# A reordered opening for a dequantizing feed-forward kernel: first-tile copies, rescales and statistics

## The chip, the cores and the metric

The kernel runs on one core of one Trainium2 chip. The metric is the device time of one execution in microseconds. A core has TensorE (PE, with its weight loads PEld), VectorE (DVE), ScalarE (ACT), GpSimd (POOL) and SyncE (SP). SP, ACT and GpSimd can each issue DMA transfers from a queue of their own; within a queue instructions are issued in order.

## The reference, cut to what matters

The input is 2 x 1024 rows of 1024 numbers, so 2048 rows. Three residual steps follow each other:

```python
x = x + 0.5 * ffn(layernorm(x))
x = x + s4(layernorm(x))
x = x + 0.5 * ffn(layernorm(x))
# ffn: h = silu(xf @ Wg) * (xf @ Wu); out = h @ Wd
# weights: W[k,n] = scales[g[k],n] * (w4[k,n] - (z4[g[k],n] + 1))
```

Wg and Wu are 1024 x 2752, Wd is 2752 x 1024. They come packed, eight 4-bit numbers in one 32-bit word, with a scale and a 4-bit zero point for each group of 128 rows of k and each column. The step in the middle, s4, convolves each row of 1024 with a response that is computed from a few small tables.

## The kernel before, in words

**Tiling.** The rows are worked through in four blocks of 512. A job is one block with one feed-forward step, and there are eight jobs, (0,1), (1,1), (0,3), (1,3), (2,1), (3,1), (2,3), (3,3): block, and 1 or 3 for the first or second feed-forward step. Each job has an **up stage** (`gate_up`, the products with Wg and Wu) and a **down stage** (`down`, the products with Wd). The s4 step of a block is laid into a later up stage.

**The weights are unpacked once.** During the first job the packed words are fetched, split into bytes (`split`, L381 and L382: the low and the high halves of every byte), and `dequantize` (L396) subtracts the zero point and writes a tile q of integers as floats. q goes to HBM (L400, tensors `wq`), and the products read it back from there as tiles w (L461). All later jobs only read. The same is done for Wd (`dequantize_down` L428, stores L430, loads L469). The scales are not multiplied in; instead a sum in PSUM is multiplied between two groups g and g+1 by the ratio of their scales (`scaled`: on ACT L477, on DVE L479), and by the last scale at the end (L523, L526).

**Waves and steps.** The up stage has eight waves of three or two column tiles of 128, and each wave eight steps g, 64 steps in all. A step has six pairs of products, one for each unit (a column tile of Wg or of Wu): with the low part (xTl) and with the high part (xTh) of the rows, both 512 wide (L501). The six sums of a wave lie in six PSUM banks. After each step but the last each unit is rescaled: units with an even number on ACT, the others on DVE, except that in job 0 the unit at position 1 is also ACT's when `g % 4 < 3`. The down stage has 44 steps of four units (L562), with the same kind of rescale.

**The buffers.** One pool of six tiles (`wpool`) holds both the q on their way to HBM and the w that were read back, and the first tile. A load of w is issued `AHEAD = 3` steps before its products.

**The first tile.** The first step's weights don't take the way through HBM: while q of wave 0 is written, the 16 partitions of q that belong to group 0 are copied from one buffer to the other, eight times 48 KB, with DMAs from ACT's queue (L399, `first_tile`).

**The opening.** In the order of the program: the zero points of all three matrices are fetched, unpacked (L220, L229), stored in HBM as a table and read back spread over the rows (L376); four tiles x of rows come in (L1163); `moments` (L137, L138) takes mean and variance of each tile and ACT subtracts the mean (L1173); `deviations` (L156 to L159) works out the reciprocal deviation r with three Newton steps on tiles of four columns; eight times `dequantize`; the first scale table (`scales`); ACT multiplies by r (L1185); TensorE transposes (L173), ACT rounds the result to the high part (L187) and DVE takes the rest as the low part (L188).

**What sets the order.** The program attaches pieces of work to steps (`at(up, s, f)`, `at(dn, s, f)`), but a planner then orders the instructions of each engine by when it thinks their operands are ready and their result is due. Work written for a later step can so come to stand earlier: the statistics of job 1's rows are written for step 0 of the first down stage, and ran from 194.9 us on, within the first up stage; the small operations on `s_vc`, which begin the tables of s4 and are written for job 1, ran from 314.8 us on in the first down stage.

Of the kernel before, what the change touches and what calls it, by code (L numbers as in the profile page):

```python
# [15 lines left out]
ALU = mybir.AluOpType  # L16
AX = mybir.AxisListType
PSUM = bass.MemoryType.PSUM
DRAM = bass.MemoryType.DRAM
# [30 lines left out]
def macaron_s4_kernel(  # L50
# [63 lines left out]
    shift_t = const.tile([P, 1], I32, tag="shift", name="shift_t")  # L114


    x = {}
# [50 lines left out]

    def turned(n, half, name, bank=bank):

        ps = bank(name)
        for k in range(4):
            nc.tensor.transpose(ps[:, bass.ts(k, P)], n[:, bass.ts(4 * half + k, P)], ident)  # L173
        return ps.rearrange("p (c t) -> p c t", c=4)
# [4 lines left out]
    def turn(b, t, n, half, bank=bank):  # L179
        k = ln[b, t][2]  # L180
        if b not in pieces:
            pieces[b] = [
                xtpool.tile([P, NC, TB], F32R, tag="xT", name=f"xT{w}_{b}_{k}") for w in ("h", "l")
            ]
        hi, lo = (a[:, 4 * half : 4 * half + 4, bass.ts(t, P)] for a in pieces[b])
        ps = turned(n, half, f"pt_{b}_{k}_{t}_{half}", bank)
        nc.scalar.copy(hi, ps)  # L187
        nc.vector.tensor_tensor(lo, ps, hi.bitcast(F32), ALU.subtract)  # L188
# [19 lines left out]

    def zero_points():

        n, nd = INTER // 8 // SEG, HID // 8 // SEGD
        z = t2("zq").bitcast(I32)[:, : n + nd]
        nc.gpsimd.memset(z, 0)
        for i, src in enumerate((gate_qz, up_qz)):
            own = slice(GK * SEG * i, GK * SEG * (i + 1))
            nc.scalar.dma_start(z[own, :n], src.rearrange("g (s n) -> (g s) n", s=SEG))
        nc.scalar.dma_start(z[: GD * SEGD, n:], down_qz.rearrange("g (s n) -> (g s) n", s=SEGD))
        zi = t4("zi").bitcast(I32)[:, : 8 * (n + nd)]
        for k in range(8):
            nc.vector.tensor_scalar(  # L220
                zi.rearrange("p (a k) -> p k a", k=8)[:, k, :],
                z,
                4 * k,
                15,
                ALU.logical_shift_right,
                ALU.bitwise_and,
            )
        tab = t2("ztab").bitcast(BF16)[:, : 8 * (n + nd)]
        nc.vector.tensor_scalar(tab, zi, 1.0, None, ALU.add)  # L229
        nc.scalar.dma_start(z_dram.rearrange("g (s n) -> (g s) n", s=SEG), tab[:, : 8 * n])  # L230
        nc.scalar.dma_start(
            zd_dram.rearrange("g (s n) -> (g s) n", s=SEGD), tab[: GD * SEGD, 8 * n :]
        )

# [156 lines left out]
    def dequantize(w, j):  # L391

        parts, z = packed[w]
        q = wpool.tile([P, width_of(w)], F32R, tag="w", name=f"q_{w}_{j}")
        src = parts[j % 2][:, j // 2, :]
        nc.vector.tensor_tensor(q, src, z, ALU.subtract)  # L396
        dst = w_q[w].rearrange("(r j) n -> j r n", j=8)[j]
        if w == 0:
            nc.scalar.dma_start(first_tile[j:P:8].bitcast(F32), q[: P // 8].bitcast(F32))  # L399
        nc.sync.dma_start(dst, q.bitcast(F32))  # L400
        if j == 7:
            packed.pop(w)
# [31 lines left out]
    def first_weights(up, dn, at):  # L434


        for w in range(1, len(WAVES)):
            s0 = 8 * w - 12
            at(up, max(0, s0 - 3), lambda w=w: (fetch(w), fetch_zeros(w)))
            at(up, max(0, s0 - 1), lambda w=w: split(w))  # L440
            for j in range(8):
                s = s0 + j if w > 1 else (1, 2, 2, 3, 3, 3, 4, 4)[j]
                at(up, s, lambda w=w, j=j: dequantize(w, j))
# [9 lines left out]

    AHEAD = 3

    def load_w(j, s):
# [24 lines left out]
    def gate_up(j, b, hooks):  # L481
        hi, lo = pieces[b]
        ps = {}
        ready = {s: load_w(j, s) for s in range(AHEAD)}
        for s, (wi, g) in enumerate(STEPS):
            if s + AHEAD < len(STEPS):
                ready[s + AHEAD] = load_w(j, s + AHEAD)
            for hook in hooks.get(s, ()):
# [7 lines left out]
            for pos, (unit, col) in enumerate(order):  # L496
# [12 lines left out]
                if g < GK - 1:  # L509
                    on_act = unit % 2 == 0 or (j == 0 and pos == 1 and g % 4 < 3)  # L510
                    if unit == 2 * WIDE:
# [333 lines left out]
    def turn_whole(n, name):  # L845
        s = t4(name).rearrange("p (c t) -> p c t", c=NC)
        for half in range(2):
            ps = turned(n, half, f"{name}_{half}")
            dst = s[:, 4 * half : 4 * half + 4, :]
            if half:  # L850
                nc.vector.tensor_copy(dst, ps)
            else:
                nc.scalar.copy(dst, ps)
# [217 lines left out]
    def fast():  # L1071
        for j, (b, k) in enumerate(JOBS):
# [47 lines left out]
            if j == 0:  # L1120
                for s, k0, k1 in ((2, 3, 11), (12, 11, 19), (20, 19, WIDE)):
                    at(up, s, lambda k0=k0, k1=k1: scales(k0, k1, scale_rows(k0, k1)))
                at(up, 28, scales_down)
                for t in range(NT):
                    at(up, t, lambda t=t: turn(0, t, first[t], 1))
                first_weights(up, dn, at)
            if j == 1:
                tables = s4_tables()
                for s in range(2, 42):
                    at(up, s, lambda: next(tables, None))  # L1130
            if j == 2:
                at(up, 30, in_order)
            if after:
                ab, ak = after
                if ak == 1:
                    at(up, 55 if j == 0 else 6, lambda: load_x(ab, rows_of(u, ab)))
                    stage, o = (dn, 0) if j == 0 else (up, 44)
                    at(stage, o, lambda: moments(ab, 1))
                    at(stage, o + 1, lambda: deviations(ab, 1))
# [4 lines left out]

                o = 3 if j == 0 else 0
                for t in range(NT):
                    at(dn, o + 1 + 4 * t, lambda t=t: anorm(t))
                    at(dn, o + 2 + 4 * t, lambda t=t: turn(ab, t, an[t], 0))
                    at(dn, o + 4 + 4 * t, lambda t=t: turn(ab, t, an[t], 1))
            at(dn, 21, lambda: load_x(b, rows_of(u, b) if k == 1 else saved(b)))  # L1150
# [8 lines left out]

    zero_points()  # L1160
    x[0] = [t4(f"x_0_{t}") for t in range(NT)]
    for t, src in enumerate(rows_of(u, 0)):
        nc.sync.dma_start(x[0][t], src)  # L1163
        if t == 1:
            fetch(0)
    fetch_zeros(0)
    srow = scale_rows(0, 3, nc.scalar)
    first = []

    def less_mean(t, m):  # L1170

        n = t4(f"xn_0_1_{t}")
        nc.scalar.activation(n, x[0][t], AF.Identity, bias=m, scale=-1.0)  # L1173
        first.append(n)
        if t == 1:
            split(0)

    moments(0, 1, less_mean)
    deviations(0, 1, -1.0)
    for i in range(8):  # L1180
        dequantize(0, i)
    scales(0, 3, srow)
    for t in range(NT + 1):
        if t < NT:
            nc.scalar.activation(first[t], first[t], AF.Copy, scale=ln[0, t][1])  # L1185
        if t:
            turn(0, t - 1, first[t - 1], 0, acc)
    x.pop(0)
# [87 lines left out]
```

## Time and profile before

| | us |
|---|---|
| time, median of 3 | 2224.56 (2221.06 to 2226.02) |
| span of the profiled execution | 2218.9, granted clock 0.995 |
| first product of job 0 (L501) | 35.44 |
| first up stage | 190.2 |
| first down stage | 102.6 |
| up stage of job 1 (with s4 of block 0 and its tables) | 214.5 |
| up stages of jobs 2, 5, 6 (with s4) | 194.6 to 196.5 |
| up stages of jobs 3, 4, 7 | 159.8 to 159.9 |
| down stages of jobs 1 to 6 | 85.9 to 86.4 |

The stages were cut at the first product of L501 or L562 of each. A stage in which TensorE is never without work has the same length each time it comes up; what the first ones have above that is waiting. In the profile an engine's busy time is the sum over its instructions, and a wait is booked to what ended it last.

### The profile page before, as it was taken

How to read it: one execution, taken by the hardware profiler on the slowest of the kernel's cores; microseconds unless marked ns; L12 is line 12 of the kernel's file. 1: busy time of each engine (PE TensorE's matmuls, PEld its weight loads, DVE VectorE, ACT ScalarE, POOL GpSimd, SP SyncE). 2: the span in 40 equal slices, each digit the busy share in tenths (PEclk: the TensorE clock that was granted, in tenths of full speed). 3: DMA queues.
4: the chain of work that ended last, by engine and by line, in shares of the span. 5: the costliest groups of instructions: out<-in, count | busy, mean ns of one | idle time of the engine just before them, and what ended most of it. 6: DMA issues, size and time to landing. Idle time of an engine off the chain costs nothing.

```text
span 2218.9 us, 28013 instructions
## 1 busy us (share of the span) xinstructions
PE 2134.2 (96%) x9364; PEld 1683.4 (76%) x9364; DVE 1712.8 (77%) x2792; ACT 1452.8 (65%) x2229; POOL 328.8 (15%) x350
## 2 busy tenths in 40 slices
PE   4898889999999999999999999999999999999998
PEld 3676667867887778888788878877788777888876
DVE  7898869767786878877887777867788677777776
ACT  5776776545764677677767777646676467767775
POOL 0232002211011230122102320102201023012210
PEclk9999999999999999999999999999999999999999
DMA  7788784434443545644455444434444354554444
GB/s 238 271 261 274 233 250 131 141 96 150 135 149 107 174 135 173 225 146 136 142 185 187 126 138 138 150 104 159 138 136 146 108 180 134 156 189 144 135 136 130
DMA packets 163667, 359.91 MB, mean 162 GB/s; under 512 B 22395, under 2 KB 27588, under 8 KB 163518
## 3 DMA queue, kind: packets, MB, share of 16 engines
q1 hardware_dynamic: 162730, 357.47, 51.8%
q8 instruction: 78, 1.28, 0.2%
q10 hardware_dynamic: 788, 0.58, 0.1%
q14 instruction: 71, 0.58, 0.1%
HBM read 306.86 MB, written 50.73 MB: 161 GB/s over the span
## 4 chain that ended last, share of the span: by engine, by line
PE 51%; issue 35%; DMA 5%; DVE 5%; POOL 3%; ACT 1%; SPq 0%; ACTq 0%; DVEq 0%; POOLq 0%
PE pg L501 35%; PE po L562 9%; PE pc L835 5%; POOL hl L530 2%; POOL hh L528 1%; DMA w<-wq 1%; DMA wd<-wdq 1%; DMA wdq<-qd 1%; DVE pg L479 1%; DVE hf L526 1%; DVE q L396 1%; PE st L173 1%; DMA wq<-q 1%; PE pt L173 0%; PE pb L583 0%
## 5 line engine op out<-in xcount | busy, mean ns | idle before, releaser
L477 ACT ACTIVATE pg<-pg,rat 128x512 f32<-128x512 f32 x1256 | 820.1, 662 | 467.0 <-PE pg L501 462.4
L501 PE MATMUL pg<-xTl,w 128*128 128x512 f32 x2752 | 1084.3, 396 | 27.9 <-DVE pg L479 12.2
L501 PE MATMUL pg<-xTh,w 128*128 128x512 f32 x2752 | 1070.9, 391 | 0.0
L479 DVE TENSOR_TENSOR pg<-pg,rat 128x512 f32<-128x512 f32 x1152 | 785.8, 696 | 162.9 <-PE pg L501 154.1
L501 PEld LDWEIGHTS pg<-xTl,w 128*128 128x128 f32 x2752 | 517.8, 188 | 164.1 <-DVE pg L479 22.6
L501 PEld LDWEIGHTS pg<-xTh,w 128*128 128x128 f32 x2752 | 518.6, 188 | 103.3 <-issue 0.2
L562 PE MATMUL po<-hl,wd 128*128 128x512 f32 x1344 | 538.2, 403 | 18.4 <-DVE po L479 7.7
L477 ACT ACTIVATE po<-po,ratd 128x512 f32<-128x512 f32 x670 | 438.7, 662 | 170.1 <-PE po L562 169.8
L562 PE MATMUL po<-hh,wd 128*128 128x512 f32 x1344 | 521.3, 392 | 0.0
L479 DVE TENSOR_TENSOR po<-po,ratd 128x512 f32<-128x512 f32 x610 | 419.1, 697 | 93.5 <-PE po L562 89.2
L528 POOL CAST hh<-hf 128x512 fp32r<-128x512 f32 x168 | 109.4, 651 | 1755.1 <-DVE hf L526 1630.5
L562 PEld LDWEIGHTS po<-hl,wd 128*128 128x128 f32 x1344 | 252.1, 188 | 96.4 <-DVE po L479 18.4
L562 PEld LDWEIGHTS po<-hh,wd 128*128 128x128 f32 x1344 | 253.4, 189 | 46.0
L530 POOL TENSOR_TENSOR hl<-hf,hh 128x512 fp32r<-128x512 f32 x168 | 222.9, 1327 | 13.5
L526 DVE SCALAR_TENSOR_TENSOR hf<-pg,rat,g 128x512 f32<-128x512 f32 x168 | 125.1, 748 | 78.6 <-PE pg L501 32.6
L523 ACT ACTIVATE g<-pg,rat 128x512 f32<-128x512 f32 x168 | 115.6, 689 | 41.8 <-PE pg L501 39.2
L835 PE MATMUL pc<-toeplitz,st 128*128 128x512 f32 (+3 forms) x384 | 126.5, 486 | 0.0
L835 PEld LDWEIGHTS pc<-toeplitz,st 128*128 128x128 f32 x384 | 70.3, 190 | 57.4 <-issue 46.0
L843 DVE TENSOR_TENSOR x<-x,pc 128x512 f32<-128x512 f32 x32 | 22.0, 686 | 77.4 <-PE pc L835 77.2
L137 DVE BATCH_NORM_STATS2 stats<-x 128x6 f32<-128x512 f32 x96 | 64.6, 679 | 2.2 <-DMA x<-in_L_attn_u_dram 1.1
L188 DVE TENSOR_TENSOR xTl<-pt,xTh 128x512 fp32r<-128x512 f32 x64 | 43.5, 685 | 17.3 <-ACT xTh L187 17.3
L173 PE MATMUL pt<-ident,xn 128*128 128x128 f32 x256 | 42.9, 286 | 14.1 <-ACT xn L1185 14.1
(135 smaller groups left out, 617.5 us busy)
## 6 DMA issues: line engine op xcount, KB each, us to landing
w<-wq SPq DMA_DIRECT2D x319, 384.0 KB
wd<-wdq SPq DMA_DIRECT2D x336, 256.0 KB
w<-wq SPq DMA_DIRECT2D x128, 256.0 KB
w<-wq SPq DMA_DIRECT2D x64, 320.0 KB
x<-in_L_attn_u_dram SPq DMA_DIRECT2D x32, 512.0 KB
wq<-q SPq DMA_DIRECT2D x40, 384.0 KB
wdq<-qd SPq DMA_DIRECT2D x32, 256.0 KB
xs<-x SPq DMA_DIRECT2D x16, 512.0 KB
```

The costliest lines, as they stand in the source:

```text
L137: nc.vector.bn_stats(stats[:, t, i, :], x[b][t][:, bass.ts(i, 512)])
L173: nc.tensor.transpose(ps[:, bass.ts(k, P)], n[:, bass.ts(4 * half + k, P)], ident)
L188: nc.vector.tensor_tensor(lo, ps, hi.bitcast(F32), ALU.subtract)
L477: nc.scalar.activation(dst, src, AF.Copy, scale=sc)
L479: nc.vector.tensor_tensor(dst, src, sc.to_broadcast([P, TB]), ALU.mult)
L501: nc.tensor.matmul(p, w[:, bass.ts(col, P)], part[:, g, :], start=(g == 0 and k == 0), stop=(g == GK - 1 and k == 1), skip_group_check=True,)
L523: nc.scalar.activation(g, pg, AF.Silu, scale=rat[:, 2 * f, GK - 1 :])
L526: nc.vector.scalar_tensor_tensor(hf, pu, last, g, ALU.mult, ALU.mult)
L528: nc.gpsimd.tensor_copy(hi, hf)
L530: nc.gpsimd.tensor_tensor(lo, hf, hi.bitcast(F32), ALU.subtract)
L562: nc.tensor.matmul(ps[c], w[:, bass.ts(c, P)], part, start=(f == 0 and k == 0), stop=(f == NF - 1), skip_group_check=True,)
L835: nc.tensor.matmul(ps[:, lo - 512 * nh :], lhsT(c), toeplitz[:, lo - P * c : end - P * c], start=(c == 0), stop=(c == last),)
```

## The change

It reorders the opening and the first job, in seven edits.

1. A helper `in_order_of_writing` pins what a piece of program writes for the named engines to the order in which it is written, one instruction after the other, so that the planner can't move it within that engine's queue. The whole opening, the second halves of the first rows and the split of wave 1 are pinned on ACT, DVE and SP; later splits on DVE, later fetches on SP; the s4 tables on DVE and ACT.
2. The opening is written anew: zero points of gate and up first, those of down apart and late (`zero_words`, `zero_points`); the tiles x 2 and 3 come in from ACT's queue; the packed words and zeros of wave 1 are fetched in the opening; the Newton steps stand ahead of all eight `dequantize`; the rows are normalized in halves of 512, first halves first, the second halves in steps 0 to 3 of the up stage.
3. The copies of the first tile go out from GpSimd's queue.
4. In job 0 ACT takes the unit at position 1 in every step: four of six rescales.
5. In job 0 a load of w is issued two steps ahead instead of three (`FIRST = 2`).
6. The scale tables are made in parts of 6, 6 and 6 tiles at steps 4, 20 and 36, not of 8, 8 and 2 at 2, 12 and 20; that of down at step 40, not 28; the unpacking of wave 1 is spread a little wider.
7. The statistics of job 1's rows are written for step 14 of the first down stage, not 0, and pinned on DVE; normalization and transposes follow from step 21, not 4.

```diff
         if w == 0:
-            nc.scalar.dma_start(first_tile[j:P:8].bitcast(F32), q[: P // 8].bitcast(F32))
+            nc.gpsimd.dma_start(first_tile[j:P:8].bitcast(F32), q[: P // 8].bitcast(F32))
...
-            at(up, max(0, s0 - 3), lambda w=w: (fetch(w), fetch_zeros(w)))
-            at(up, max(0, s0 - 1), lambda w=w: split(w))
+            if w > 1:
+                both = lambda w=w: (fetch(w), fetch_zeros(w))
+                at(up, s0 - 3, lambda both=both: in_order_of_writing(both, ET.SP))
+                at(up, s0 - 1, lambda w=w: in_order_of_writing(lambda: split(w), ET.DVE))
+            else:
+                at(up, 0, lambda: in_order_of_writing(lambda: split(1), *STARTING))
             for j in range(8):
-                s = s0 + j if w > 1 else (1, 2, 2, 3, 3, 3, 4, 4)[j]
+                s = s0 + j if w > 1 else (1, 2, 2, 3, 3, 4, 4, 5)[j]
...
+    FIRST = 2
...
-        ready = {s: load_w(j, s) for s in range(AHEAD)}
+        ahead = AHEAD if j else FIRST
+        ready = {s: load_w(j, s) for s in range(ahead)}
...
-                    on_act = unit % 2 == 0 or (j == 0 and pos == 1 and g % 4 < 3)
+                    on_act = unit % 2 == 0 or (j == 0 and pos == 1)
...
-                for s, k0, k1 in ((2, 3, 11), (12, 11, 19), (20, 19, WIDE)):
+                for s, k0, k1 in ((4, 3, 9), (20, 9, 15), (36, 15, WIDE)):
...
-                at(up, 28, scales_down)
+                at(up, 40, scales_down)
                 for t in range(NT):
-                    at(up, t, lambda t=t: turn(0, t, first[t], 1))
+                    at(up, t, lambda t=t: in_order_of_writing(lambda: second_half(t), *STARTING))
...
                 for s in range(2, 42):
-                    at(up, s, lambda: next(tables, None))
+                    piece = lambda: next(tables, None)
+                    at(up, s, lambda: in_order_of_writing(piece, ET.DVE, ET.Activation))
...
-                    stage, o = (dn, 0) if j == 0 else (up, 44)
-                    at(stage, o, lambda: moments(ab, 1))
+                    stage, o = (dn, 14) if j == 0 else (up, 44)
+                    at(stage, o, lambda: in_order_of_writing(lambda: moments(ab, 1), ET.DVE))
...
-                o = 3 if j == 0 else 0
+                o = 20 if j == 0 else 0
...
+    STARTING = ET.Activation, ET.DVE, ET.SP
...
+    def start():
+        zeros = zero_words(0)
+        x[0] = [t4(f"x_0_{t}") for t in range(NT)]
+        for t, src in enumerate(rows_of(u, 0)):
+            (nc.sync, nc.scalar)[t // 2].dma_start(x[0][t], src)
+        fetch(0)
+        srow = scale_rows(0, 3)
+        zeros_down = zero_words(1)
+        fetch(1)
+        zero_points(0, zeros)
+        fetch_zeros(0)
+        fetch_zeros(1)
...
+        moments(0, 1, then)
+        deviations(0, 1, -1.0)
+        for i in range(8):
+            dequantize(0, i)
+        for t in range(NT + 1):
+            if t < NT:
+                by_deviation(t, 0)
+            if t:
+                turn(0, t - 1, first[t - 1, 0], 0, acc)
+        for t in range(NT):
+            less_mean(t, 1)
+        scales(0, 3, srow)
+        zero_points(1, zeros_down)
+
+    in_order_of_writing(start, *STARTING)
```

## The prediction

> **What bounds the kernel now.** I read the granted clock first (0.995), then the 40 slices, then the span cut at the first product of every stage, and last the chain, the waits and the timelines of the first two stages. The stage table decides where time can be won (columns: span; busy us and count for PE, weight loads, DVE, ACT, POOL; clock; DMA share; GB/s):
>
> ```profile
> 35.40:225.70 190.30, 171.62 (x724) 129.30 (x724) 163.64 (x252) 140.95 (x224) 47.88 (x40) 0.99 0.80 267
> 225.70:328.30 102.60, 91.92 (x393) 68.03 (x393) 78.02 (x160) 75.48 (x123) 2.01 (x3) 0.98 0.76 238
> 911.60:1071.50 159.90, 159.38 (x705) 130.19 (x705) 123.05 (x182) 114.93 (x174) 35.42 (x38) 1.00 0.53 167
> 1071.50:1158.00 86.50, 85.57 (x394) 68.41 (x393) 72.33 (x123) 59.15 (x93) 3.71 (x4) 1.00 0.53 161
> ```
>
> The third and fourth rows are a later up stage and down stage, with TensorE full. The first up stage takes 190.3 us against 159.9, the first down stage 102.6 against 86.5: 30.4 and 16.1 us above the floor of the same products, because the weights are unpacked there, stored to HBM and read back. Before them lie 35.4 us without a product. From job 1 on the change touches almost nothing, so all it can win is in these 82 us.
>
> The opening, from the timelines of ACT and DVE and the chain of waits:
>
> ```profile
> 17.34 10.04 ACTq L399 DMA_DIRECT2D w<-q  x8
> 27.48 3.23 ACT L1185 ACTIVATE xn<-xn,r 128x1024 f32<-128x1024 f32 x3 [11.42 <-DMA w<-q]
> ```
> ```profile
> 23.38 0.95 DVE L396 TENSOR_TENSOR q<-raw,z 128x768 fp32r<-128x768 uint8 x1
> 25.43 0.16 DVE L159 TENSOR_SCALAR r<-r 128x4 f32<-128x4 f32 x1
> ```
> ```profile
> 22.99 4.47 DMA w<-q
> 27.48 1.16 ACT xn L1185
> 28.64 0.04 issue
> 28.68 5.37 PE pt L173 x24
> ```
>
> ACT issues eight copies of the first weight tile, 10.04 us long, and only then scales the rows; and the deviation r itself is late (25.6 us), since its small operations lie between the eight unpackings. The transposes start at 28.68 and the first product at 35.44.
>
> In the first up stage the path is mixed (of 190 us: PE 87.8, DMA 47.4, DVE 34.8, ACT 7.9). The queue's own waits tell why DMA stands there:
>
> ```profile
> SPq L400 <- DVE q L396: 67.1, 46, 3.9
> SPq L461 <- DMA wq<-q: 13.2, 10, 3.8
> SPq L461 <- PE pg L501: 12.7, 22, 2.1
> ```
>
> One queue carries stores and loads in order: it stands 67.1 us for DVE's unpacking, and the loads of the next weights stand behind it. So DVE bounds this stage at second hand (busy 163.6 of 190.3 us), DMA traffic (share 0.80) next.
>
> **What the Trainium skill says.** *DMA: Bandwidth & Descriptors*, "Issuing engines are not separate DMA queues": all queues end on the same 16 DMA engines, and another issuer saves only issue time. The trace agrees in that the price was ACT's 10.04 us, not bytes (8 x 48 KB). The same page, "Anatomy of one DMA — SWDGE (gpsimd) path", fits 2.0 us + bytes/436e3 for GpSimd's own descriptors: 2.1 us for 48 KB. No run here shows a DMA from GpSimd; before, its queue is empty. *SBUF — State Buffer*, "Who interferes with whom": DVE in a 2-port mode locks GpSimd out of writing descriptors; a two-input operation isn't in such a mode. The unpackings are two-input (0.95 us for 768), only the splits (0.54 us for 768) aren't. *TensorE: Matmul & The Clock Gate*, Part 1: after idling, TensorE's clock falls to half, and some 3.4 us of activity bring it back. The trace agrees in the length, though the gap is shorter than the page's idle window: after 2.04 us without a product before 209.92, products take 0.63 us instead of 0.39 from 211.5 to 214.5.
>
> **The start, part by part.** (a) *r first.* The down zeros leave the first table: it waits for two loads and covers 43 words instead of 75, so it ends near 7.4 us instead of 8.2. Four statistics at 1.4 us (8.12, 9.56, 10.95, 12.35) and two splits (1.1) end at 14.1; then 14 dependent small operations at 0.195 us (231.06, 231.26, 231.45, 231.65) give r at 16.8 instead of 25.6. (b) *ACT freed.* Half rows cost 0.6 us; four scalings and four roundings end about 22, the transposes between them. (c) *Zeros.* In the compiled order, ACT's store of the zero table now also waits for the last of the rows x to land, whose completion semaphore it reuses. Rows and packed weights are 2.5 MB; at 306 GB/s (the rate from 2 to 6 us) from 2.0 us they land at 10.4. Store 4.12 us as in the chain (or 2.5 with less traffic), load 0.74 + 3.03: unpacking begins between 16.7 and 18.3; I take 17.6, later than 16.35 before. (d) Eight unpackings at 0.87, and 0.7 for the sixth, which reuses the buffer of the first and waits for its store: 25.3. (e) Four remainders at 0.65: 27.9. (f) *GpSimd's copies.* The last is issued at 25.3. Lower bound 2.1 us, upper 4.47 (the last ACT copy in the chain) + 1: 27.4 to 30.8; I take 29.5, so the first product goes from 35.4 to 29.5. (g) The second tile must be stored and loaded: 25.3 + 0.3 + 4.1, issue at 30, 4 us of landing: 34. Before, its first product ran at 38.2. **The start gives 4.2 us** (2.5 to 6), not the 6 of the first product.
>
> **First up stage.** ACT takes unit 1 in every step, before in three of four: steps g = 3 of eight waves, 8 rescales x 0.60 us start to start = 4.8 us off DVE; on ACT 8 x 0.62 = 5 us, hidden, as ACT is busy 141 of 190. Statistics of the next rows ran here at 194.9 to 224.7 though written for the down stage; pinned at down step 14 they take 8 x 0.64 + 4 x 0.13 + 0.9 = 6.5 us along. DVE loses 11.3 of 163.6 us. Lower bound of what that gives: DVE's share of the path, 34.8/190 x 11.3 = 2; upper: 11.3 x 190.3/163.6 = 13. I take 8, since the queue's 67.1 us make most of DVE's time count. *Two tiles ahead instead of three:* a step is 12 x 0.227 = 2.7 us, so the lead is 5.4 us; loads on the path land in 28.2/6 = 4.7 us. It lets the queue not stand 13.2 us for stores on their way, and gives q one more buffer, but uncovers any load slower than 5.4. I take 0 (5 won to 10 lost). The scale tables in three parts of six at steps 4, 20, 36 only move about the same work; 0.
>
> **First down stage.** In come 6.5 us of statistics, at a step where rows are unpacked; out go some 30 small operations of the response tables (L625 to L693, 0.15 to 0.29 us), about 6 us, now pinned in the next up stage, and the chain of L156/L157, for which products waited 1.9 us. Normalization moves from step 4 to 21, away from the unpacking. I take 2 us won (3 lost to 7 won). The next up stage gets those 6 us of DVE with products limited by PE (210 of 214.5): +0.5 (0 to 4).
>
> **Sum**: -4.2 - 8 - 2 + 0.5 = -13.7: 2224.6 - 13.7 = **2211 us**.
>
> **Rivals.** *Start only:* the first stage is held by its traffic (190.3 us at 267 GB/s, 51 MB), and what DVE gives is lost in DMA: -4.2 to -5.5, 2219 to 2220. For: a DMA share of 0.78 to 0.88 in every window from 75 to 226 us. Against: shares of 0.96 to 0.99 and up to 349 GB/s were reached from 20 to 26 us. *All of it:* DVE's 13, 5 from the freed queue, 7 down, start 5: 2195. For: the half-clock spells vanish too. Against: path shares. *Slower:* the shorter lead uncovers loads. Waits for w are 7.0 + 3.1 us in products and weight loads now; three times that, with start 4 and DVE 4 kept, is +12: 2236. For: the longest loads on the path, 5.75 and 6.45 us, exceed 5.4. Against: more room for q brings stores forward. *Nothing:* GpSimd's copies trail to 34 us and pinned DVE work waits where it could have passed: 2224.
>
> **Chances.** Forecast 0.45, start only 0.20, all 0.18, slower 0.10, nothing 0.07. Faster by over 0.2% (under 2220.1): 0.45 + 0.18 + most of start only = 0.80; within: 0.11; slower: 0.09. The range 2194 to 2224 leaves out the slower case and the edge of the best.
>
> **What would show it.** First product near 29.5 and second tile's near 34; r near 17 and ACT with no wait of 11 us; the eight GpSimd copies each about 2 to 4 us from issue to landing; first up stage about 182 us, with fewer waits of the queue for stores; down stage about 100; job 1's up stage within 1 us of 214.5. Wrong if the waits for w grow beyond 10 us, if the zero table's store lands after 16 us, or if the first up stage keeps 190 us although DVE has 11 less.

## The result, and the profile after

The change makes the kernel slower. Measured beside the kernel before on the same chip it took 2234.65 us (median of 4, 2230.74 to 2237.85) against 2222.81 (median of 4, 2219.59 to 2226.02): a ratio of 1.0052 with a 95% interval of 1.0029 to 1.0076, about 12 us. The forecast was 2211.

The stage rows of the changed kernel (columns as before: span; busy us and count of PE, weight loads, DVE, ACT, POOL; clock; DMA share; GB/s) are the first up stage, the first down stage, job 1's up stage and job 3's up stage:

```profile
30.54:227.02 196.48, 173.67 (x727) 133.83 (x728) 148.15 (x229) 146.10 (x235) 42.91 (x38) 0.97 0.81 263
227.02:334.54 107.52, 95.08 (x393) 68.56 (x393) 82.38 (x144) 74.68 (x123) 4.43 (x4) 0.97 0.73 234
334.54:553.33 218.79, 212.54 (x885) 160.37 (x884) 166.96 (x332) 118.18 (x182) 36.96 (x41) 0.98 0.41 125
921.53:1083.19 161.66, 160.78 (x705) 129.54 (x704) 129.61 (x205) 114.06 (x174) 35.87 (x38) 1.00 0.54 165
```

The start is 4.9 us shorter. Every row after it is longer than before: the first up stage by 6.3 us, the first down stage by 4.9, job 1's up stage by 4.3, and the up stages of jobs 3 and 4 by 1.8 and 3.0 (162.8 us in job 4). All other stages agree within 0.6 us. Start and stages together come to +14.6, the difference of the two profiled executions. DVE is indeed relieved in the first up stage, 148.2 us busy instead of 163.6, and the stage is longer all the same.

The lines have moved in the changed kernel. What is needed below: L158 and L159 are the statistics, L177 to L180 the Newton steps and r, L423 is the unpacking, L427 the store of q, L436 and L441 fetch the packed words and zeros of Wd, L457 stores the unpacked Wd, L493 is the load of w, L509 and L511 are the rescales on ACT and DVE, L534 is the product. The chain of the changed kernel, from r to the first products (start, us, what):

```profile
16.25 0.17 DVE r L179
16.52 2.71 DVE q L423 x3
19.23 0.28 issue
19.51 4.68 DMA w<-q
24.27 0.97 DVE q L423
25.23 0.28 issue
25.51 4.89 DMA w<-q
30.54 4.13 PE pg L534 x10
```

r comes when it was forecast, and the unpacking begins right behind it and ends when it was forecast. What is new is that GpSimd's copies stand in the chain twice. The two of 48 KB that stand there took 4.7 and 4.9 us to land. The last one holds the first product. An earlier one holds the eighth unpacking, which waits for the buffer that is being copied.

The queue's waits in the first up stage of the changed kernel (total us, times, longest) are the lines that the forecast leaned on:

```profile
SPq L427 <- DVE q L423: 67.9, 45, 4.9
SPq L493 <- DMA wq<-q: 13.2, 8, 4.8
SPq L493 <- PE pg L534: 12.9, 22, 2.1
```

They stood at 67.1, 13.2 and 12.7 before. Fifteen us less of DVE and a load issued one step later have changed none of them. What grew is the products' own wait for weights, 7.0 us before:

```profile
PE pg L534 <- DMA w<-wq: 16.8, 9, 5.0
PE pg L534 <- DMA w<-q: 3.6, 1, 3.6
```

The stage can be followed by the start of every n-th product of the first up stage (96 make a wave in the first five waves). These starts, in us, were read from the traces' matmul records:

| n | 0 | 12 | 48 | 96 | 144 | 480 | 544 | 608 | 687 |
|---|---|---|---|---|---|---|---|---|---|
| before | 35.4 | 38.3 | 48.1 | 62.7 | 74.8 | 162.0 | 180.2 | 199.9 | 223.3 |
| after | 30.5 | 35.5 | 46.5 | 63.9 | 77.8 | 162.7 | 183.3 | 206.8 | 226.8 |

The head start of 4.9 us is gone at product 96, the first of wave 1: wave 0 takes 33.4 us instead of 27.3. Its first 12 products lose 2.1 us of this, and at its end the products wait for the first tile of wave 1. DVE unpacks its last piece at 56.04, the store goes out at 57.02, and the load, which waits for that store to land, at 59.39 (DVE, SP's queue, PE):

```profile
56.04 0.95 DVE L423 TENSOR_TENSOR q<-raw,z 128x768 fp32r<-128x768 uint8 x1
57.02 1.79 SPq L427 DMA_DIRECT2D wq<-q  x2
59.39 0.82 SPq L493 DMA_DIRECT2D w<-wq  x2
63.90 0.77 PE L534 MATMUL pg<-xTl,w 128*128 128x512 f32 x1 [3.89 <-DMA w<-wq]
```

Between products 480 and 608 another 6.2 us go, but from 608 to the end of the stage the changed kernel takes 20.2 us instead of 25.8, so 5.6 of them come back. The net loss of the stage, 6.3 us, is about that of wave 0. The second place can be read line by line. On SP's queue of the changed kernel the first packed words of Wd are fetched at 191.84:

```profile
191.84 0.42 SPq L436 DMA_DIRECT2D rawd<-_L_ffn_down_qweight_dram  x1
192.31 0.61 SPq L441 DMA_DIRECT2D zd<-zd_dram  x1
192.96 1.19 SPq L145 DMA_DIRECT2D x<-in_L_attn_u_dram  x2
199.10 0.33 SPq L457 DMA_DIRECT2D wdq<-qd  x1
199.53 0.38 SPq L493 DMA_DIRECT2D w<-wq  x1
```

DVE waits for these words until 197.42. The queue waits 4.9 us for DVE, from 194.15 to 199.10. The load of w behind that store goes out at 199.53, and PE shows the end of it:

```profile
203.30 0.76 PE L534 MATMUL pg<-xTl,w 128*128 128x512 f32 x1 [5.02 <-DMA w<-wq]
```

The matmuls then run at half clock: 0.76 us for the first and 0.63 for the next, which start 0.43 us apart, against 0.39 and 0.23 in full flow. Before the change the same words were fetched at 164.43 and their zeros at 173.71, and no such wait is there.

### The profile page after: what moved, and what is told of

The parts are those of the page before. It is cut to its first block, busy times and chain, and to the rows that moved or that the text cites. A ratio compares the mean times of both kernels' runs of the same rounds, so it can differ in the third digit from the quotient of the medians.

```text
span 2233.5 us, 28027 instructions
## 1 busy us (share of the span) xinstructions
PE 2144.2 (96%) x9364; PEld 1686.5 (76%) x9364; DVE 1707.7 (76%) x2793; ACT 1455.6 (65%) x2245; POOL 329.2 (15%) x357
## 4 chain that ended last, share of the span: by engine, by line
PE 62%; issue 25%; DVE 5%; POOL 3%; DMA 3%; ACT 1%; SPq 0%; ACTq 0%; DVEq 0%; POOLq 0%
PE pg L534 39%; PE po L595 16%; PE pc L868 5%; POOL hl L563 2%; POOL hh L561 1%; DVE pg L511 1%; DMA wd<-wdq 1%; PE pb L616 1%; DMA w<-wq 1%; DVE hf L559 1%; PE st L194 1%; DVE q L423 1%; PE pt L194 1%; DMA wdq<-qd 0%; DMA w<-q 0%
## 5 line engine op out<-in xcount | busy, mean ns | idle before, releaser
L509 ACT ACTIVATE pg<-pg,rat 128x512 f32<-128x512 f32 x1264 | 822.9, 662 | 478.9 <-PE pg L534 474.9
L534 PE MATMUL pg<-xTl,w 128*128 128x512 f32 x2752 | 1085.8, 398 | 38.7 <-DMA w<-wq 17.1
L534 PE MATMUL pg<-xTh,w 128*128 128x512 f32 x2752 | 1070.9, 392 | 0.0
L511 DVE TENSOR_TENSOR pg<-pg,rat 128x512 f32<-128x512 f32 x1144 | 781.4, 695 | 168.2 <-PE pg L534 158.8
L534 PEld LDWEIGHTS pg<-xTl,w 128*128 128x128 f32 x2752 | 519.3, 189 | 179.4 <-ACT pg L509 21.5
L534 PEld LDWEIGHTS pg<-xTh,w 128*128 128x128 f32 x2752 | 520.5, 189 | 103.8 <-issue 0.2
L595 PE MATMUL po<-hl,wd 128*128 128x512 f32 x1344 | 540.7, 404 | 16.5 <-DVE po L511 9.0
L509 ACT ACTIVATE po<-po,ratd 128x512 f32<-128x512 f32 x670 | 437.9, 662 | 168.4 <-PE po L595 167.8
L511 DVE TENSOR_TENSOR po<-po,ratd 128x512 f32<-128x512 f32 x610 | 420.0, 698 | 98.5 <-PE po L595 94.4
L158 DVE BATCH_NORM_STATS2 stats<-x 128x6 f32<-128x512 f32 x96 | 63.6, 676 | 1.2
L194 PE MATMUL pt<-ident,xn 128*128 128x128 f32 x256 | 43.0, 285 | 12.7 <-ACT xn L1205 10.4
```

Source lines behind the costliest of these rows:

```text
L158: nc.vector.bn_stats(stats[:, t, i, :], x[b][t][:, bass.ts(i, 512)])
L194: nc.tensor.transpose(ps[:, bass.ts(k, P)], n[:, bass.ts(k, P)], ident)
L509: nc.scalar.activation(dst, src, AF.Copy, scale=sc)
L511: nc.vector.tensor_tensor(dst, src, sc.to_broadcast([P, TB]), ALU.mult)
L534: nc.tensor.matmul(p, w[:, bass.ts(col, P)], part[:, g, :], start=(g == 0 and k == 0), stop=(g == GK - 1 and k == 1), skip_group_check=True,)
L595: nc.tensor.matmul(ps[c], w[:, bass.ts(c, P)], part, start=(f == 0 and k == 0), stop=(f == NF - 1), skip_group_check=True,)
```

## The experiments

All times are medians. "Against before" is the ratio to the runs of the kernel before on the same chip, with its interval; us are that ratio less one, times 2222.8. The versions ran on several chips, so the difference of two versions is the difference of two such ratios. One profile gives the first up stage only roughly: the changed kernel and e3, whose order of instructions there is the same, took 196.5 and 201.2 us. So times decide on an edit, and stages only tell where to look.

| version | median us | against before | us | first up | first down |
|---|---|---|---|---|---|
| changed kernel | 2234.65 | 1.0052 [1.0029, 1.0076] | +11.6 | 196.5 | 107.5 |
| e1 three tiles ahead | 2237.97 | 1.0072 [1.0058, 1.0086] | +16.0 | 202.7 | 103.2 |
| e2 statistics free | 2226.89 | 1.0019 [1.0012, 1.0026] | +4.2 | 196.5 | 104.1 |
| e3 tables of s4 free | 2234.42 | 1.0043 [1.0030, 1.0057] | +9.6 | 201.2 | 108.8 |
| e4 ACT three of four | 2232.07 | 1.0038 [1.0024, 1.0051] | +8.4 | 196.8 | 105.7 |
| e5 fetches free | 2233.43 | 1.0038 [1.0025, 1.0050] | +8.4 | 195.1 | 109.1 |
| e6 old steps | 2242.76 | 1.0089 [1.0075, 1.0103] | +19.8 | 206.7 | 107.1 |
| e7 free, old steps, two ahead | 2217.05 | 0.9967 [0.9954, 0.9980] | -7.3 | 190.1 | 104.9 |
| e8 the same, three ahead | 2226.00 | 1.0008 [1.0000, 1.0016] | +1.8 | 198.1 | 102.2 |
| e9 as e7, new steps | 2222.48 | 1.0003 [0.9995, 1.0011] | +0.7 | 196.9 | 103.0 |
| e10 before, two ahead | 2228.21 | 1.0029 [1.0019, 1.0040] | +6.4 | 192.4 | 102.3 |
| e11 as e7, ACT three of four | 2214.55 | 0.9972 [0.9963, 0.9982] | -6.2 | 187.6 | 102.9 |
| e12 as e7, copies from ACT | 2219.52 | 0.9995 [0.9985, 1.0004] | -1.1 | 190.4 | 103.3 |
| e13 before, new opening | 2226.64 | 1.0026 [1.0016, 1.0035] | +5.8 | 196.9 | 104.7 |
| e14 as e11, wave 1 earlier | 2230.10 | 1.0052 [1.0037, 1.0066] | +11.6 | 200.4 | 102.6 |
| e15 as e7, tables late | 2226.22 | 1.0028 [1.0017, 1.0039] | +6.2 | 199.7 | 103.2 |
| e16 before, ACT every step | 2223.54 | 1.0016 [1.0010, 1.0023] | +3.6 | 192.2 | 101.2 |
| e17 as e7, fetches pinned | 2231.45 | 1.0039 [1.0025, 1.0053] | +8.7 | 208.3 | 103.5 |
| e18 as e7, splits pinned | 2233.92 | 1.0052 [1.0034, 1.0069] | +11.6 | 206.6 | 102.6 |

### One edit of the changed kernel undone

**e1, the lead.**

```diff
-        ahead = AHEAD if j else FIRST
+        ahead = AHEAD
-                s = s0 + j if w > 1 else (1, 2, 2, 3, 3, 4, 4, 5)[j]
+                s = s0 + j if w > 1 else (1, 2, 2, 3, 3, 3, 4, 4)[j]
```

> The changed kernel with the weights of job 0 loaded three steps ahead again instead of two (and the unpackings of wave 1 at their old steps, which a lead of three needs). Theory of the short lead: the products' waits for w (20.4 us in the first up stage, 7.0 before) fall to about 7 and the stage from 196.5 to 184-187 us; time 2222-2225. Rival, the loss lies in the order of DVE's and the queue's work: the waits keep their sum or change their name, stage 194-197 us, time 2232-2236.

The products' waits for w fell from 20.4 to 13.5 us, and the time did not fall (+16.0 us against +11.6, intervals overlapping). The theory of the short lead is not borne out: what the loads gave, other waits took, among them ACT's for a late scale table, 10.8 us. The wave change itself did better (product 96 at 59.8 instead of 63.9). The run isn't a clean test of the lead, as it also moves the unpacking of wave 1, which has a price of its own (e15 against e9 below).

**e2, the statistics.**

```diff
-                    stage, o = (dn, 14) if j == 0 else (up, 44)
-                    at(stage, o, lambda: in_order_of_writing(lambda: moments(ab, 1), ET.DVE))
+                    stage, o = (dn, 0) if j == 0 else (up, 44)
+                    at(stage, o, lambda: moments(ab, 1))
...
-                o = 20 if j == 0 else 0
+                o = 3 if j == 0 else 0
```

> The changed kernel with the statistics of the next job's rows free again for the planner, everywhere, and written for step 0 of the first down stage, normalization from step 4, as before. Theory that pinned statistics cost where they stand: first down stage from 107.5 back to 102-103 us, the up stages of jobs 3 and 4 from 161.7 and 162.8 to 160 us, the first up stage up by no more than 3 (they go back into it); time 2224-2227. Rival, they only displace: what the down stage gains the first up stage loses again, time 2232-2236.

The theory holds. The first down stage is 3.5 us shorter, though not down to the 102 to 103 expected, and the up stages of jobs 3 and 4 are back at 159.9 and 159.8. The first up stage keeps its length. That is 7.4 us of the 11.6, the largest loss that undoing one edit takes away. In jobs 3 and 4 it is the pin alone, as the place is the same; in the first down stage pin and place were undone together. In the changed kernel, DVE in job 3's up stage shows the pinned chain:

```profile
1041.60 0.70 DVE L511 TENSOR_TENSOR pg<-pg,rat 128x512 f32<-128x512 f32 x1 [0.21 <-PE pg L534]
1042.21 1.28 DVE L158 BATCH_NORM_STATS2 stats<-x 128x6 f32<-128x512 f32 x2
1043.40 0.68 DVE L511 TENSOR_TENSOR pg<-pg,rat 128x512 f32<-128x512 f32 x1
1043.99 0.20 DVE L159 BATCH_NORM_AGGREGATE mv<-stats 128x2 f32<-128x12 f32 x1
1044.11 1.23 DVE L158 BATCH_NORM_STATS2 stats<-x 128x6 f32<-128x512 f32 x2
1045.26 0.68 DVE L511 TENSOR_TENSOR pg<-pg,rat 128x512 f32<-128x512 f32 x1
```

Ahead of the statistics, DVE rescales every 0.91 us and waits 0.2 us for each product. From 1042.21 to 1049.68 the pinned chain puts two statistics between each two rescales, which then come every 1.86 us. The products feel it just behind, where the small operations that lead to r follow: products 544 to 575 of this stage take 8.6 us instead of 7.3. Before the change single statistics ran spread over the following down stage, from 1086 to 1097.

**e3, the tables of s4**, and **e4, ACT's share**:

```diff
-                    at(up, s, lambda: in_order_of_writing(piece, ET.DVE, ET.Activation))
+                    at(up, s, piece)
```

> The changed kernel with the tables of s4 no longer pinned to their order on DVE and ACT. Theory that pinning costs job 1: its up stage from 218.8 to 214.5 us, time 2230. Rival, job 1 is longer since the work moved into it, pinned or not, or free tables go back into the first down stage and lengthen that: time 2233-2236.

Job 1's up stage fell from 218.8 to 213.4, a little below before. The time fell by only 2 us with overlapping intervals, as the first down stage took 1.2 more and the first up stage was long in this profile. So the cost in job 1's stage is shown; its worth in time is not.

```diff
-                    on_act = unit % 2 == 0 or (j == 0 and pos == 1)
+                    on_act = unit % 2 == 0 or (j == 0 and pos == 1 and g % 4 < 3)
```

> The changed kernel with unit 1 of job 0 on ACT in three steps of four, as before. Theory that ACT's second rescale in a row holds up the products (weight loads wait 12.1 us for ACT): first up stage from 196.5 to 192-194 us, time 2230-2232. Rival, the relief of DVE is a gain that other losses hide: first up stage 200-205 us, time 2238-2243. Third, the stage is held by transfers: no difference over 1.5 us.

The first up stage stayed (196.8) with DVE 4 us busier. With +8.4 instead of +11.6 us, intervals overlapping, giving ACT the work was at best nothing.

**e5, the fetches**, and **e6, the steps**:

```diff
-                at(up, s0 - 3, lambda both=both: in_order_of_writing(both, ET.SP))
+                at(up, s0 - 3, both)
```

> The changed kernel with the fetches of the packed words (waves 2 to 7) no longer pinned on the queue. In the changed kernel the first words of Wd are fetched 54 loads of w after the start of the queue, before the change after 43 to 47; here after 46. Theory: the late fetch makes DVE, then the queue's store, then the loads behind it wait (4.9 us at the store, 10 us of products without w from 192 to 204); with fetches free, products 480 to 608 take 38 to 40 us instead of 44.1, the first up stage 190 to 193, time 2228-2231. Rival, the wait there comes from the rows x that are loaded in the same place and from traffic: it stays, 2233-2236.

Products 480 to 608 took 38.5 us instead of 44.1, as expected, and PE's waits for w there fell from 10.0 to 4.3 us. So the late fetch did cause that wait. The stage won only 1.4 us of it, since the 79 products behind took 25.5 instead of 19.9: most was given back within the stage. The time fell by 3 us, with overlapping intervals.

```diff
-                s = s0 + j if w > 1 else (1, 2, 2, 3, 3, 4, 4, 5)[j]
+                s = s0 + j if w > 1 else (1, 2, 2, 3, 3, 3, 4, 4)[j]
...
-                for s, k0, k1 in ((4, 3, 9), (20, 9, 15), (36, 15, WIDE)):
+                for s, k0, k1 in ((2, 3, 11), (12, 11, 19), (20, 19, WIDE)):
...
-                at(up, 40, scales_down)
+                at(up, 28, scales_down)
```

> The changed kernel with the scale tables and the unpacking of wave 1 at their old steps. Theory: the last unpacking of wave 1 stands behind the scale table at step 4 and at step 5 itself, so the first tile of wave 1 comes late (3.9 us without w at 59.6 and half clock after it); with the old steps wave 0 takes 29 us instead of 33.4, and the first up stage is 3 to 5 us shorter, time 2229-2232. Rival, with two tiles ahead the change of waves stays uncovered whatever the steps: wave 0 keeps 32-34 us, time 2233-2236.

Both expectations failed in time: 8 us slower still, intervals just touching. Wave 0 kept 32.3 us, as the rival said, but waves 1 to 3 took 29.6, 27.4 and 28.5 us instead of 24.9, 24.2 and 24.5. With the pins the old steps are the worse ones.

### Pins off, one part at a time

**e7 and e8** free statistics, tables, fetches and splits and take the old steps (the diffs of e2, e3, e5 and e6 together, and `split(w)` unpinned). The opening, its copies and ACT's four of six stay. e8 adds three tiles ahead.

> Keeps of the change the opening, the copies from GpSimd, ACT's four of six and two tiles ahead; statistics, tables, splits and fetches are free for the planner, and all steps are the old ones. If losses add up as found so far (statistics 7.5, late fetch 4.5, wave change 4, tables 0 to 4), 2215-2220, the first up stage 186-189. Rival, two tiles ahead cost on their own: 2222-2228.

> The same with three tiles ahead. Theory of the short lead: 3 us or more faster than with two, 2211-2217. Rival, the lead is indifferent or the freer queue is worth more: 2216-2222, within 2 us of the version with two.

e7 beats both kernels: 7 us faster than before, 19 faster than the change. Its time is as expected; its first up stage was to be shorter (186 to 189). For e8 both expectations failed: of the two leads the shorter one is better here, by 9 us. With three ahead the waits for w were fewer (6.1 against 10.0 us), but the products' waits for DVE's rescales rose from 2.7 to 8.5. The first up stage of e7:

```profile
30.55:220.61 190.06, 172.96 (x728) 134.35 (x728) 153.01 (x253) 146.03 (x235) 42.43 (x38) 0.98 0.82 272
```

DVE is 5 us busier in it than in the changed kernel and the stage 6 us shorter.

**e9 and e15** put the new steps back into e7: e9 both groups, e15 the scale tables alone.

> As the free version with two tiles ahead (2217.1 us), but with the scale tables and the unpacking of wave 1 at the steps of the changed kernel. So against the changed kernel only the pinning outside the opening and the place of the next rows' statistics are undone. If pinning and statistics are the whole loss: within 2 us of 2217, first up stage 188-191. If the new steps cost on their own (a table of scales at step 4, the last unpacking of wave 1 at step 5): 2220-2224, the loss within products 48 to 144.

> As the free version with two tiles ahead (2217.1 us), but the scale tables at the later steps of the changed kernel (4, 20, 36, and 40 for down). If the late tables cost, since they meet the first words of Wd there: 2220-2223 and products 480 to 544 take 21 us or more instead of 17.5. If the later steps of wave 1 cost instead: 2216-2218.

e9 is the changed kernel without the pins on fetches, later splits, tables and statistics, and with the statistics in their old place; the opening, the second halves and the split of wave 1 stay pinned. It takes as long as the kernel before (+0.7 us). So these pins and the moved statistics are 10.9 of the 11.6 us that the change lost, and the intervals don't overlap.

e9 is 8 us and e15 13.5 us slower than e7, so the late tables cost in this order. Where they cost is less clear. Products 480 to 544 took 24.5 and 23.3 us instead of 17.5, but the next 64 took 16.1 and 15.8 instead of 18.6, and e15 lost 10 us in waves 1 to 4 against 4 won in wave 0. The loss of e9 was expected between products 48 and 144, and is not there. In e15 SP's queue issues 3.7 us of zeros and rows between two loads of w (177.33 to 180.99), and the products wait 3.4 us for w at 185.80; but e7's queue has such a run of 4.3 us too (162.37 to 166.68), and its products then wait for no w before 180. How the tables lead to the loss stays open. The later steps of wave 1, which e9 has and e15 hasn't, are a gain here: e9 is 5 us faster than e15.

**e17 and e18** put one pin back into e7: fetches on SP, or splits on DVE.

> As the free version with two tiles ahead (2217.1 us), but the fetches of packed words pinned on the queue. In this order zeros of Wd's first words come after 54 loads of w instead of 43, and the words of wave 3 after 11 instead of 5 loads. If the pinned fetches are the cause of the missing 25 us: 2232-2242, first up stage 200 or more. If they are one of two: 2221-2230.

> The same with the splits of waves 2 to 7 pinned on VectorE instead. If pinning an operation of VectorE holds up what is written after it there: 2225-2240. If the planner's place for the splits is as good as the written one: 2216-2220.

Each alone takes 16 and 19 us, and the first up stage grows to 208 and 207. In e17 the products' wait for w is 22.9 us, against 10.0. They don't add: the version with both, the other pins and the moved statistics (e6) is at +19.8 us. So of the 27 us between e6 and e7 fetches or splits, each by itself, are enough for more than half.

**e11** gives e7 the old share of ACT, **e12** copies the first tile from ACT's queue.

> As the free version with two tiles ahead (2217.1 us), but unit 1 on ACT in three steps of four, as before. My prediction's term, DVE's relief of 4.8 us shortens the stage: 2220-2222. Rival, what the queue waits for is the pace of the steps and not DVE's busy time, so the relief is worth nothing: 2215-2218.

> As the free version with two tiles ahead (2217.1 us), but the first tile is copied from ACT's queue. Theory, GpSimd's copies cost a landing of 5 us and half clock after it, ACT's cost ACT eight issues of 1.25 us: first product at 30-33 instead of 30.5, time within 2 us of 2217. Rival, ACT's issues hold up the normalization as they did before: first product at 35, time 2219-2222 if the head start counts, 2217 if the first change of waves takes it anyway.

e11 equals e7 within the intervals (0.9972 against 0.9967): relieving DVE by 4.8 us is worth nothing in this order either. In e12 the first product came at 34.70 instead of 30.55, and the time rose by 6 us, so GpSimd's queue is a gain for the copies in this order. ACT's view of e12 shows the wait of the kernel before come back:

```profile
17.49 10.36 ACTq L426 DMA_DIRECT2D w<-q  x8
27.89 1.33 ACT L1205 ACTIVATE xn<-xn,r 128x512 f32<-128x512 f32 x2 [12.81 <-DMA w<-q]
```

### One part of the change alone

**e10, e13 and e16** are the kernel before with one part each: two tiles ahead; the new opening; unit 1 on ACT in every step. **e14** is e11 with the unpacking of wave 1 at steps `(0, 1, 1, 2, 2, 2, 3, 3)`.

> The kernel before with nothing but two tiles ahead instead of three in job 0. If the shorter lead is a gain of its own (9 us in the free versions): 2213-2217. If it only suits the new opening: 2220-2226. If it uncovers loads, as my slower rival said: 2227-2236, waits for w above 15 us.

> The kernel before with the new opening alone (first tile's copies from GpSimd included), three tiles ahead, ACT three of four. My prediction's term: 4.2 us, so 2217-2219. Rival, the head start goes at the change from wave 0 to wave 1, since the unpacking of wave 1 is paced by the same steps: wave 0 takes 31-34 us instead of 27.3, time 2221-2226.

> The kernel before with nothing but unit 1 on ACT in every step of job 0. My prediction: 8 rescales of 0.60 us off DVE, 2 to 6 us faster, 2216-2220. Rival, DVE's busy time does not set the stage: within 1.5 us of before. Third, the planner arranges queue and DVE anew and the time moves either way by up to 5 us with the waits for w.

> As the free version with ACT three of four (2214.6 us), but the unpacking of wave 1 written one step earlier (steps 0 to 3). If the pace of that unpacking takes the head start at the first change of waves: wave 0 takes 30-32 us instead of 35.1, time 2210-2213. Rival, DVE or the buffers are taken in the first steps anyway: the products wait for DVE instead, wave 0 keeps 34-36 us, time 2213-2217.

Each of the three parts alone makes the kernel slower, by 6.4, 5.8 and 3.6 us: together, in e7, they make it 7.3 us faster. The runs with two of them tell more. Opening and short lead without ACT's share are e11, at -6.2 us; opening and ACT's share without the short lead are e8, at +1.8. So the opening and the short lead are enough for the gain: the short lead costs 6.4 us in the order of before and is worth 12.0 with the new opening (e13 to e11). In e10 the products' waits for w rose from 7.0 to 11.1 us, not to the 15 that the third expectation named. In e13 the first product starts at 30.3, product 96 at 59.9, and product 144 at 78.0 against 74.8 before: the gain is lost in wave 1, not in wave 0 as the rival said. There DVE has the unpacking of wave 2 and a scale table ahead of a rescale, and the products stand:

```profile
68.22 0.80 PE L534 MATMUL pg<-xTl,w 128*128 128x512 f32 x1 [3.75 <-DVE pg L511]
```

In e14 products 24 to 48 took 11.9 us instead of 9.4 and wave 0 kept 33.7 us, as its rival said, but the time, that of the changed kernel, is far beyond both expectations. Unpacking earlier is no cure.

## Why the prediction was wrong

The sum was -13.7 us, and +11.6 was measured. Two versions lie on the way. e7 keeps the opening, ACT's share and the short lead, and has -7.3. e9 adds the new steps, which I had put at 0, and has +0.7: 8.0 us lost. The changed kernel adds the pins that e9 lacks and the moved statistics, in which I had seen a gain, and has +11.6: 10.9 us lost. These shares hold for this way only; in the pinned kernel the new steps are worth 8 us the other way (e6).

**The start** came to its first product about as forecast, in part by luck, and was wrong in its worth. r came at 16.6 (16.8 forecast), and ACT had no wait of 11 us. The unpackings ended at 25.2 (25.3), but two errors cancel there. They began at 16.5 right behind r, and not at 17.6 behind the zeros: the store of the zero table went out at 10.51 and the loads behind it at 12.34, so it took under 1.9 us and not 4.12. And they took 8.7 us and not 7.7: the sum lacks the eighth's wait of 0.96 us for a buffer that was still being copied. The copies landed in 4.8 us in the median, where I had said 2 to 4. The 4.47 us that I took for the last ACT copy were a misreading: they begin at 22.99 with the issue of the sixth, and the eighth is issued from 25.85 to 27.38. The first product came at 30.54, near the upper bound of 30.8. The second tile's first product came at 35.50, not 34, and not for its store and load: 12 products took 5.0 us instead of 2.9, as PE had stood 3.6 us and started at half clock, 0.63 us for each of the next products (as after the stands of 3.9 and 5.0 us above), and then waited 0.38 us for a rescale on ACT. So 2.8 of the 4.2 us were there. The step that failed is the one after it: that a head start stays. It was gone at product 96, and the opening alone is 5.8 us slower (e13). In e7, too, product 96 starts later than before, at 65.4 against 62.7, and e7 is ahead only behind product 288 (at product 384 it is 137.5 against 138.6). Measured against e12, which has e7's order, starts 4.2 us later and is 6 us slower, e7's start does count.

**The first up stage** is where the forecast broke: "DVE loses 11.3 of 163.6 us" was right in direction (15.4 measured), but "I take 8, since the queue's 67.1 us make most of DVE's time count" was wrong: the stage grew by 6.3 us. The queue's 67.1 us were no measure of DVE's load. With DVE 15 us emptier the wait was 67.9, and DVE stood 28.9 us for products instead of 14.8. My reading, which no run tests by itself, is that the queue waits for a tile that is unpacked once a step, between rescales that themselves wait for products. DVE's busy time and the stage don't go together: 148 us in 196.5 (the change), 153 in 190.1 (e7), 158 in 187.6 (e11), 165 in 196.9 (e13). The relief by ACT's part alone has no fixed worth: nothing clear of noise in e4 and e11, a loss of 3.6 us in e16, and a gain of 4.0 between e13 and e8, which differ in nothing else, with intervals that just touch.

**Prefetch** counted 0, from 5 won to 10 lost. In e7's order 9 us were won, more than the bound allowed, and 6.4 were lost in that of before: the sign depends on the order, and lead against landing time doesn't give it. The 7.0 + 3.1 us of waits for w counted the same stretches twice, as each wait of a weight load lies at the wait of its product.

**Scale tables** "only move about the same work; 0" was wrong with no bounds given: 13.5 us in e15, and 8.0 together with the new steps of wave 1 in e9.

**The pins** on fetches, splits and statistics I counted at nothing, without a reason. With the moved statistics they are 10.9 of the 11.6 us (e9). In the free version a single pin costs 16 or 19 us (e17, e18). In the changed kernel, undoing the fetches' pin alone gave 3, with overlapping intervals.

**The first down stage** should have won 2 us and lost 4.9; 3.5 of these are the statistics, by pin or place (e2). **Job 1** should have lost 0.5 (0 to 4) and lost 4.3, all of it gone without the pin on the tables (e3).

**What I did not read** in the diff: the pin of `moments` holds for every job, not for job 0 alone. "From job 1 on the change touches almost nothing" missed 1.8 and 3.0 us in jobs 3 and 4, where PE had no slack.

**The rivals.** "Slower: the shorter lead uncovers loads", 2236, came nearest in time, and the waits for w did grow, to 20.4 us. Its cause is not borne out: with the longer lead (e1) the waits fell and the kernel was no faster, though e1 moves wave 1 as well; with pins and statistics undone and the short lead kept (e9) the loss is gone. "Nothing" named the pinned DVE work that waits, for which e2 and e18 found a price, but it saw no net loss. "Start only" falls, since the start is worth nothing in the order of before. What stays open is why the opening and the short lead each lose alone and win together. My reading is that the planner places stores, fetches and rescales anew after each edit; I have shown where single waits come from, not a rule for the sum.

## What to carry to other kernels

A queue that waits long for an engine doesn't show that the engine is short of time: ask first whether the wait changes with its load, and look at what the engine itself waits for. A pin of order is a change of its own, with a price: on an in-order engine it lines up operations that a planner had spread, and on a shared queue it delays what is written after it. Where edits rearrange a planned order, their single effects don't add, so build the sum from combinations, and leave the parts out one by one from the version that wins. Look at whole stages: what is lost at one place can come back behind it.

## What the hardware showed that I had not expected

**Copies from GpSimd's queue.** The DMA view of the changed kernel from 16 to 31 us (packets, MB and share of 16 engines for each kind of queue; then count, KB each and median us from issue to landing):

```profile
q1 hardware_dynamic: 1269, 3.21, 57.6%
q0 software_dynamic: 256, 0.39, 19.2%
...
w<-q POOLq DMA_DIRECT2D x8, 48.0 KB, 4.8
```

The Trainium skill, *DMA: Bandwidth & Descriptors*, "Anatomy of one DMA — SWDGE (gpsimd) path", gives a fit from which 2.1 us is the estimate for 48 KB. Here it was 4.8, beside 3.2 MB of other traffic; the measurement decides. The trace has no landing for ACT's copies before, so whether the queue or the traffic makes the difference is not shown. What GpSimd's queue saves is issue time: its eight issues took 0.48 to 0.65 us each, ACT's before 10.0 us together. Per MB the copies took 49% of the 16 engines' time in that stretch, the other packets 18%. Most of this lies in the copies and not in the queue: from ACT's queue, in the same stretch of the kernel before, they took 13.6% for 0.39 MB, 35% per MB.

**DVE and GpSimd block each other.** In e13, in the same stretch in which the products wait for DVE in wave 1, DVE's and then GpSimd's timeline read:

```profile
62.21 2.04 DVE L423 TENSOR_TENSOR q<-raw,z 128x768 fp32r<-128x768 uint8 x1
64.18 1.36 DVE L423 TENSOR_TENSOR q<-even,z 128x768 fp32r<-128x768 uint8 x1
```
```profile
62.15 1.29 POOL L563 TENSOR_TENSOR hl<-hf,hh 128x512 fp32r<-128x512 f32 x1
63.38 1.34 POOL L561 CAST hh<-hf 128x512 fp32r<-128x512 f32 x1
```

An unpacking alone takes 0.95 us, a cast on GpSimd 0.61. GpSimd's subtraction, which started first, takes its usual 1.29 us and ends at 63.44; 63.44 + 0.87 of unpacking (from start to start) is 64.3, near the end of the first row, 64.25. The cast, issued at 63.38, ends 0.5 us after that, at 64.72, and DVE's second row ends 0.82 us later. These times fit operations that ran in turn. The Trainium skill, *SBUF — State Buffer*, "Who interferes with whom", says so of DVE operations with two inputs in SBUF beside GpSimd operations that read SBUF: whoever issues first blocks the other. The times in the trace agree. I had used that section for the copies and not for the unpackings, which lose some 1.5 us to it here, ahead of the rescale for which PE waits at 68.22.
